# Cross-attention on one core: normalization in two halves, an earlier transposition of the probabilities, and two buffers for x

## The chip, the core and the metric

The kernel runs on one core of a Trainium2 chip. A core has five engines with a queue of instructions each: TensorE (PE, matrix products; its weight loads are listed as PEld), VectorE (DVE), ScalarE (ACT), GpSimd (POOL) and SyncE (SP), which here only issues DMAs. Each queue runs in order; engines wait for one another through semaphores. Sixteen DMA engines move data between the chip's memory (DRAM) and the on-chip memory; matrix products land in PSUM, eight banks of 2 KB per partition. The metric is the device time of one execution in microseconds (us). The time before is 1811.44 us, the median of three runs (1804.13 to 1816.82).

## The reference

A cross-attention block: 32 batches of 512 queries with 640 channels, 20 heads of 32 channels, and 77 context rows of 1024 channels for each batch. The reference also has weights for three further groups of context rows (object, others, ip), but the context has only the 77 text rows, so those groups are empty and add nothing.

```python
q = _heads(x @ to_q_w)                                # 32 x 512 x 640
k, v = _heads(ctx @ to_k_w), _heads(ctx @ to_v_w)     # 32 x 77 x 1024 -> 640
s = jnp.einsum('bhqd,bhkd->bhqk', q, k) / sqrt(32)
p = jax.nn.softmax(s, axis=-1)
h = _merge(jnp.einsum('bhqk,bhkd->bhqd', p, v))
out = h @ to_out_w + to_out_b + x
```

All data is 32-bit. The products with weights are made more exact by splitting both operands into a high and a low part and adding three products (high x high, high x low, low x high).

## The kernel before

**First stage (to about 250 us).** Twelve matmuls on zeros (line 253) start PE. Keys and values of all batches are computed in groups of 512 context rows (lines 177 to 220) and put into DRAM (`k_dram`, `v_dram`). The split weights of the output projection go to DRAM as well and come back later (`wos`, line 592). The values of the last group are computed inside the first two slots (`beside`).

**Slots.** The main part is a list of 160 slots, `slot(n)` for n = 0 to 159. Slot n handles batch b = n // 5 and the chunk j = n % 5 of 128 channels, which is four heads. The order of instructions is written out by hand: the program text of `slot` is the order on each engine. In a slot, in program order:

- `scores(n)` (line 410): 32 small matmuls into four PSUM tiles `sc`, one for each head, 512 queries as four blocks t of 128 partitions.
- `values(n - 3)` (line 478): probabilities (`raw`, keys in partitions) times values, for a chunk three slots back (`LAG`), into the one PSUM tile `pa`.
- `maxima(n)` (line 422): DVE takes the row maxima of the four heads.
- DMA issues on SP: `load_p(n - 2)` (line 470) reloads the probabilities of chunk n - 2 from DRAM; then keys, values of the batch, x, the residual (`xr`, line 504), as the slot has them.
- `add_bias` (line 508) on POOL, on a residual loaded a slot or more before.
- `piece` (line 515): the first half of the slot's share of the output projection of an earlier batch.
- `exps` (line 432) on ACT: for heads 0 and 1, 8 instructions with the row sums as a second result; they write `pn`, a tile of 128 x 16 x 80 with rows t * 4 + head, one of two by the parity of n.
- `transpose_p(n - 1)` (lines 454 and 461): DVE transposes the previous chunk's normalized probabilities in 32 x 32 blocks into the single tile `z`; then SP issues four DMAs that write it to a DRAM tile `pd` with keys as rows.
- `finish` (lines 544 to 550): DVE adds PSUM and residual for each block of the output that a piece has closed; SP stores complete rows. A block is 128 queries by 320 channels; the tables `STEPS` and `CUTS` say which piece closes which. In slots with j = 0, 1 and 3 the second piece closes one block, with j = 2 and 4 none; an output row is complete behind the second piece where j is 0 or 1.
- `transpose_x` (line 235) on DVE for j = 0 and 1: x of the next batch, in place in its buffer `xs`.
- `queries(n + 1)` (line 393): 15 matmuls for the next chunk's queries; `copy_q` (line 402) takes them to `qt`, on ACT, or on DVE in the first seven slots (`filling`: batches whose output projection has not begun).
- `exps` for heads 2 and 3, then `sums` (line 442, DVE reciprocal of all 16 row sums) and `normalize` (line 447, POOL multiplies all of `pn`, 1232 elements in each partition).
- `high_a`, `low_a` (lines 492 and 497): ACT and DVE split the values product.
- the second piece, `split_x` for j = 2 and 3 (lines 242 and 243, ACT high part, POOL low part, five chunks c of the next batch's x into `xt`), the remaining `transpose_x`, and `finish`.

`xs` has one buffer and `xt` seven tiles of one chunk each. All four quarters of the x of batch b + 2 are loaded in slot j = 4 of batch b. After the last slot, `end` transposes and reloads what is left and finishes the last projection.

The lines that set the order around the change are in `slot`, lines 585 to 640; in it `turns` holds what `transpose_x` is called for and `taken` is n - 3.

Of the kernel before, what the change touches and what calls it, by code (L numbers as in the profile page):

```python
# [8 lines left out]
F32 = mybir.dt.float32  # L9
# [28 lines left out]
def kernel(  # L38
# [185 lines left out]
    def load_x(b, quarters=range(4)):  # L224

        if b not in xss:
            xss[b] = xpool[0].tile([P, S // Q, C // 4], F32, tag="xs", name="xs")
        xs = xss[b]
        src = x[b].rearrange("(a j) (q u) -> q j a u", j=Q, q=4)
        for q in quarters:  # L230
            nc.sync.dma_start(xs[q * Q : (q + 1) * Q, :, :], src[q])  # L231

    def transpose_x(b, i):
        part = xss[b][:, 4 * i : 4 * i + 4, :].rearrange("p a u -> p (a u)")
        nc.vector.transpose(part, part)  # L235

    def split_x(b, c, high=nc.scalar.copy, low=nc.gpsimd):

        xt = xpool[0].tile([P, 2, S], FPR, tag="xt", name="xt", bufs=7)
        src = xss[b].rearrange("p (a t) u -> p t a u", t=NQ)[:, :, :, c * Q : (c + 1) * Q]  # L240
        parts = [xt[:, i, :].rearrange("p (t a j) -> p t a j", t=NQ, j=Q) for i in range(2)]
        high(parts[0], src)  # L242
        low.tensor_tensor(parts[1], src, parts[0].bitcast(F32), ALU.subtract)  # L243
        xts[b, c] = xt
# [4 lines left out]
    zero = kvt.tile([P, G], FPR, name="zero")  # L249
    nc.vector.memset(zero.bitcast(F32), 0.0)  # L250
    warm = psk.tile([P, G], F32, tag="ps", name="warm")
    for _ in range(12):
        nc.tensor.matmul(warm, zero[:, :P], zero, start=True, stop=True)

    def first(*ks):
# [106 lines left out]


    main = ctx.enter_context(tc.tile_pool(name="main", bufs=1, reuse_waits="tile"))
    ps = ctx.enter_context(tc.tile_pool(name="ps", bufs=1, space=PSUM, reuse_waits="tile"))
    psv = tc.alloc_tile_pool(name="psv", bufs=3, space=PSUM, side="right", reuse_waits="tile")
    late = []
# [10 lines left out]
        nc.gpsimd.memset(pn, 0.0)  # L378
        pnb.append(pn)
    qts = [main.tile([P, S], F32, name=f"qt{n}") for n in range(2)]  # L380
    z = main.tile([P, NBLK, NQ, Q], F32, name="z")
    def load_keys(b):
        nc.sync.dma_start(kbs[b % 2], k_dram[:, :, b * NKEY : (b + 1) * NKEY])

# [34 lines left out]
    def maxima(n):  # L419
        nms[n] = main.tile([P, HPC, NQ], F32, tag="nm", name="nm", bufs=2)  # L420
        for i, sc in enumerate(scs[n]):
            nc.vector.tensor_reduce(  # L422
                nms[n][:, i], sc[:, :, :NKEY], AX.X, ALU.max, negate=True
            )
# [12 lines left out]
                accum_out=sms[n][:, at : at + 1],  # L437
            )

    def sums(n):  # L440
        rss[n] = main.tile([P, NQ * HPC], F32, tag="rs", name="rs", bufs=2)
        nc.vector.reciprocal(rss[n], sms.pop(n))  # L442

    def normalize(n):
        rs = rss.pop(n)
        pf = pnb[n % 2][:, :, :NKEY]
        nc.gpsimd.tensor_tensor(  # L447
            pf, pf, rs.unsqueeze(2).to_broadcast([P, NQ * HPC, NKEY]), ALU.mult
        )

    def transpose_p(n):

        pn = pnb[n % 2]
        nc.vector.transpose(  # L454
            z.rearrange("p b t j -> p t b j"),
            pn.rearrange("p (t h) k -> p t (h k)", t=NQ).rearrange("p t (b i) -> p t b i", i=Q),
        )
        pd = dram.tile([NBLK * Q, S], F32, tag="pd", name="pd", bufs=6)
        rows = pd.rearrange("(b i) q -> i b q", i=Q)
        for a in range(4):  # L460
            nc.sync.dma_start(  # L461
                rows[:, :, a * P : (a + 1) * P],
                z[a * Q : (a + 1) * Q].rearrange("p b t j -> p b (t j)"),
            )
        pds[n] = pd

    def load_p(n):
        pd = pds.pop(n)
        raw = late[0].tile([KPAD, HPC, S], F32, tag="raw", name="raw", bufs=2)
        nc.sync.dma_start(raw, pd.rearrange("(h k) q -> k h q", h=HPC))  # L470
        raws[n] = raw
# [87 lines left out]
    PIECES = {2: (1, 0), 3: (1, 2), 4: (1, 4), 0: (2, 6), 1: (2, 8)}  # L559
    RESIDUAL = {1: (1, 0), 2: (1, 1), 3: (1, 2), 4: (1, 3)}  # L560
    BIAS = {2: (1, 0), 3: (1, 1), 4: (1, 2), 0: (2, 3)}
    TRANSPOSE_X = {0: ((0,), (1,)), 1: ((2,), (3,))}
    SPLIT_X = {2: (0, 1), 3: (2, 3, 4)}

    WO = {1: (0, 1, 2), 2: (3,), 3: (4,)}
# [2 lines left out]
    def take(m):  # L568
        values(m)
        high_a(m)  # L570
        low_a(m)

    def slot(n, beside=()):
        b, j = divmod(n, NC_)
        ahead, more = n + 1 < N, b + 1 < B
        back, first = PIECES[j]
        bo_, has_out = b - back, b >= back
        xsplits = SPLIT_X.get(j, ()) if more and n > LATE else ()
        turns = TRANSPOSE_X.get(j, ((), ())) if more and b else ((), ())
        if b == 1 and j < 2:  # L580
            turns = (((), ()), ((0, 1), (2, 3)))[j]
        taken = takes.get(n)
        filling = not has_out

        scores(n)
        if taken is not None:
            values(taken)
        maxima(n)
        if n - LAG + 1 in pds and n > LATE:
            load_p(n - LAG + 1)  # L590
        for k in WO.get(n, ()):
            nc.sync.dma_start(wos[0][:, k].bitcast(F32), wo_dram[:, k].bitcast(F32))
        if j == 0 and more:
            load_keys(b + 1)
        if j == 1:
            load_values(b)
        if n == NC_:
            load_x(b + 1, (2, 3))
        if j == 4 and b and b + 2 < B:
            load_x(b + 2, (0, 1))  # L600
        if j in RESIDUAL and b >= RESIDUAL[j][0]:
            load_residual(b - RESIDUAL[j][0], RESIDUAL[j][1])
        if j in BIAS and b >= BIAS[j][0]:
            add_bias(b - BIAS[j][0], BIAS[j][1])
        if has_out:
            piece(bo_, first)
        for i in range(2):
            exps(n, i)
        if n:
            transpose_p(n - 1)  # L610
        finish()
        if j == 4 and b + 2 < B:
            load_x(b + 2, (0, 1) if not b else (2, 3))
        for i in turns[0]:
            transpose_x(b + 1, i)
        if len(beside) > 1:
            context_values(LAST, beside[1], psv)
        if ahead:
            queries(n + 1)
        if len(beside) > 0:  # L620
            context_values(LAST, beside[0], psv)
        if filling and ahead:
            copy_q(n + 1, nc.vector.tensor_copy)
        for i in range(2, HPC):
            exps(n, i)
        sums(n)
        normalize(n)
        if taken is not None:
            high_a(taken)
        if has_out and ahead:  # L630
            copy_q(n + 1)
        if has_out:
            piece(bo_, first + 1)
        if taken is not None:
            low_a(taken)
        for c in xsplits:
            split_x(b + 1, c)
        for i in turns[1]:
            transpose_x(b + 1, i)
        finish()  # L640

    def end():


        last = B - 1
        load_p(N - 2)
        add_bias(last - 1, 3)
        piece(last - 1, 6)
        finish()
        transpose_p(N - 1)  # L650
        load_p(N - 1)
        load_residual(last, 0)
        load_residual(last, 1)
        piece(last - 1, 7)
        finish()
        take(N - 3)
        piece(last - 1, 8)
        piece(last - 1, 9)
        finish()
        load_residual(last, 2)  # L660

        def begin(i, j0, j1):
            t, h = divmod(i, 2)
            if j0 == 0:
                if i < 4:
                    pos[last, t, h] = ps.tile([P, S], F32, tag="sc", name="po", bufs=4)
                elif i == 4:
                    pos[last, t, h] = ps.tile([P, S], F32, tag="pq", name="po", bufs=1)
                elif i < 7:
                    output_bank(last, t, h)  # L670
                else:
                    pos[last, t, h] = late[1].tile([P, S], F32, tag="pa", name="po", bufs=1)
            for j in range(j0, j1):
                project(last, t, h, j)

        for i in range(2):
            begin(i, 0, 2)
        take(N - 2)
        for t in (0, 1, 2):
            add_bias(last, t)  # L680
# [88 lines left out]
```

## Time and profile before

| | us |
|---|---|
| median of three runs | 1811.44 |
| lowest and highest | 1804.13, 1816.82 |
| the profiled execution | 1809.79 |
| its span (first to last instruction) | 1808.0 |
| mean granted clock of PE in it | 0.987 |
| ACT, exponentials waiting for maxima (line 432) | 379.6 |
| POOL, normalization waiting for the reciprocal (line 447) | 659.9 |
| POOL, bias waiting for the residual (line 508) | 85.9 |
| DVE, transposition of x waiting for its load (line 235) | 74.2 |
| SP, x load waiting for the split of x (line 231) | 67.8 |

The lower rows are idle time of an engine just before the named work, summed, with what ended it. Idle time of an engine that is not the bottleneck costs nothing by itself. In rows of the profile, `L447 POOL` is the instruction of line 447 on GpSimd, `pn<-pn,rs` its output and inputs, and `x160` its count; in a timeline the first two numbers are start and duration in us, and the bracket holds the engine's idle time before it and what ended that. `SPq` is the queue of SyncE that issues DMAs. The granted clock is 1 at full speed.

### The profile page before, as it was taken

To read this page: it belongs to the slowest core of one execution; us is meant where nothing else is said; L and a number is where in the kernel's file an instruction comes from. 1 tells how busy PE (TensorE), PEld (TensorE's weight loads), DVE (VectorE), ACT (ScalarE), POOL (GpSimd) and SP (SyncE) were. 2 spreads that over 40 slices of the span, in tenths; PEclk is the share of its full clock that TensorE was granted. 3 is DMA by queue.
4 is the path that set the end of the run, shared out by engine and by line. 5 is a ranking of instruction groups with operands and counts; after the bars stand their busy time and mean duration, and the time that the engine had idled before them with its cause. 6 is when DMAs were issued, how large, how long until landed. Compare 5 with 4: busy or idle time off the path is not lost.

```text
span 1808.0 us, 39341 instructions
## 1 busy us (share of the span) xinstructions
PE 1763.3 (98%) x13852; PEld 1440.0 (80%) x13852; DVE 933.3 (52%) x1651; ACT 1108.9 (61%) x5698; POOL 789.7 (44%) x502
## 2 busy tenths in 40 slices
PE   8999998899999999999999999999999999999999
PEld 7888896678878888877788777888788888877787
DVE  5233134555555555555555555555555555545553
ACT  3132035666767777767677776677676777666662
POOL 0000034444445555545555545545555555535453
PEclk9999999999999999999999999999999999999999
DMA  9746465899999999998999999998899999898987
GB/s 186 149 94 174 105 168 138 211 231 235 232 232 239 232 243 235 240 235 219 237 232 237 228 230 237 230 233 230 229 234 230 229 240 237 229 224 219 236 207 202
DMA packets 465173, 389.12 MB, mean 215 GB/s; under 512 B 91280, under 2 KB 372368, under 8 KB 464976
## 3 DMA queue, kind: packets, MB, share of 16 engines
q1 hardware_dynamic: 462384, 379.49, 84.5%
q0 software_dynamic: 2496, 6.97, 1.3%
q8 instruction: 109, 1.79, 0.4%
q14 instruction: 88, 0.72, 0.1%
q10 hardware_dynamic: 96, 0.16, 0.0%
HBM read 223.82 MB, written 162.70 MB: 214 GB/s over the span
## 4 chain that ended last, share of the span: by engine, by line
PE 63%; DMA 17%; ACT 6%; POOL 6%; SPq 4%; DVE 2%; issue 2%; POOLq 0%; DVEq 0%; ACTq 0%
PE po L515 20%; PE pq L393 17%; PE pk L177 7%; PE pv L177 7%; DMA raw<-pd 6%; DMA pd<-z 6%; ACT pn L432 6%; PE sc L410 5%; PE pa L478 5%; POOL xt L243 4%; DMA xs<-in_x_dram 4%; SPq L461 2%; POOL pn L447 1%; SPq L231 1%; DVE xs L235 1%
## 5 line engine op out<-in xcount | busy, mean ns | idle before, releaser
L432 ACT ACTIVATE pn<-sc,nm 128x77 f32<-128x77 f32 x2560 | 787.4, 361 | 400.2 <-DVE nm L422 379.6
L515 PEld LDWEIGHTS po<-wo_s,at 128*128 128x128 f32 x3840 | 582.7, 190 | 143.8 <-issue 132.1
L447 POOL TENSOR_TENSOR pn<-pn,rs 128x1232 f32<-128x1232 f32 x160 | 364.0, 2275 | 665.1 <-DVE rs L442 659.9
L515 PE MATMUL po<-wo_s,at 128*128 128x320 f32 x3840 | 636.8, 316 | 0.0
L432 ACT ACTIVATION_READ_ACCUMULATOR pn<-sc,nm 128x1 f32 x2560 | 618.7, 242 | 0.0
L393 PE MATMUL pq<-xt,wq_s 128*128 128x512 f32 x2400 | 582.8, 395 | 0.0
L393 PEld LDWEIGHTS pq<-xt,wq_s 128*128 128x128 f32 x2400 | 450.1, 190 | 92.8 <-issue 4.9
L422 DVE TENSOR_REDUCE nm<-sc 128x4 f32<-128x308 f32 x640 | 261.0, 469 | 202.2 <-PE sc L410 202.1
L454 DVE STREAM_TRANSPOSE z<-pn 128x1280 f32<-128x1280 f32 x160 | 241.1, 1507 | 97.8 <-DMA pd<-z 92.3
L508 POOL TENSOR_TENSOR xr<-xr,bias 128x640 f32<-128x640 f32 x128 | 200.8, 1569 | 94.2 <-DMA xr<-in_x_dram 85.9
L243 POOL TENSOR_TENSOR xt<-xs,xt 128x512 fp32r<-128x512 f32 x160 | 200.0, 1274 | 35.6 <-ACT xt L242 35.6
L478 PE MATMUL pa<-raw,vb 80*32 80x512 f32 x1280 | 173.4, 613 | 27.6 <-DMA raw<-pd 19.6
L410 PEld LDWEIGHTS sc<-kb,qt 32*128 32x128 f32 x5120 | 157.5, 186 | 41.0 <-issue 35.1
L410 PE MATMUL sc<-kb,qt 32*128 32x77 f32 x5120 | 181.0, 277 | 8.7 <-DVE rs L442 5.8
L544 DVE TENSOR_TENSOR xr<-po,xr 128x320 f32<-128x320 f32 x256 | 117.5, 469 | 79.4 <-PE po L515 75.7
L235 DVE STREAM_TRANSPOSE xs<-xs 128x640 f32<-128x640 f32 x128 | 105.8, 832 | 74.2 <-DMA xs<-in_x_dram 74.2
L442 DVE RECIPROCAL rs<-sm 128x16 f32<-128x16 f32 x160 | 38.8, 243 | 196.3 <-ACT pn L432 196.3
L177 PE MATMUL pk<-ct,wk_s 128*128 128x512 f32 (+1 forms) x600 | 136.0, 387 | 3.1 <-ACT wk_s L89 3.1
L402 ACT COPY qt<-pq 128x512 f32<-128x512 f32 x153 | 93.3, 610 | 72.5 <-PE pq L393 72.1
L177 PE MATMUL pv<-ct,wv_s 128*128 128x512 f32 (+1 forms) x600 | 133.9, 381 | 0.0
L177 PEld LDWEIGHTS pk<-ct,wk_s 128*128 128x128 f32 x600 | 114.2, 191 | 23.2 <-ACT wk_s L89 3.6
L497 DVE TENSOR_TENSOR at<-pa,at 128x512 fp32r<-128x512 f32 x160 | 108.6, 679 | 37.2 <-ACT at L492 37.1
(31 smaller groups left out, 536.7 us busy)
## 6 DMA issues: line engine op xcount, KB each, us to landing
pd<-z SPq DMA_DIRECT2D x640, 160.0 KB, 5.4
raw<-pd SPq DMA_DIRECT2D x160, 640.0 KB, 5.5
xs<-in_x_dram SPq DMA_DIRECT2D x128, 320.0 KB, 6.0
xr<-in_x_dram SPq DMA_DIRECT2D x128, 320.0 KB, 5.7
out_dram<-xr SPq DMA_DIRECT2D x127, 320.0 KB, 3.9
vb<-v_dram SPq DMA_DIRECT2D x32, 200.0 KB, 6.0
kb<-k_dram SPq DMA_DIRECT2D x32, 192.5 KB, 7.3
cs<-in_ctx_dram SPq DMA_DIRECT2D x12, 512.0 KB, 9.4
```

Of the source, the lines that this page charges most:

```text
L177: nc.tensor.matmul(held[j][:, :gn], w[:, k, a, :], cts[g, k][:, c, :gn], start=(k == 0 and n == 0), stop=(k == NK - 1 and n == 2),)
L235: nc.vector.transpose(part, part)
L243: low.tensor_tensor(parts[1], src, parts[0].bitcast(F32), ALU.subtract)
L393: nc.tensor.matmul(pqs[n], wq_s[:, k, a, j * P : (j + 1) * P], xts[b, k][:, c, :], start=(k == 0 and m == 0), stop=(k == NC_ - 1 and m == 2),)
L410: nc.tensor.matmul(sc[:, t, :NKEY], qts[n % 2][r, t * P : (t + 1) * P], kbs[b % 2][r, j, :], start=True, stop=True, tile_position=(i * HD, 0),
L422: nc.vector.tensor_reduce(nms[n][:, i], sc[:, :, :NKEY], AX.X, ALU.max, negate=True)
L432: nc.scalar.activation(pnb[n % 2][:, at, :NKEY], sc[:, t, :NKEY], AF.Exp, bias=nms[n][:, i, t : t + 1], accum_out=sms[n][:, at : at + 1],)
L447: nc.gpsimd.tensor_tensor(pf, pf, rs.unsqueeze(2).to_broadcast([P, NQ * HPC, NKEY]), ALU.mult)
L454: nc.vector.transpose(z.rearrange("p b t j -> p t b j"), pn.rearrange("p (t h) k -> p t (h k)", t=NQ).rearrange("p t (b i) -> p t b i", i=Q),)
L478: nc.tensor.matmul(pas[n][i * HD : (i + 1) * HD, :], vb[:, i, :], raw[:, i, :], start=True, stop=True, tile_position=(0, i * HD),)
L508: nc.gpsimd.tensor_tensor(xrs[b, t], xrs[b, t], bias, ALU.add)
L515: nc.tensor.matmul(pos[b, t, h][:, :HALF], ats[b * NC_ + j][:, a, t * P : (t + 1) * P], wos[0][:, j, c, h * HALF : (h + 1) * HALF], start= ...
```

## The change

Eight edits in one version:

- `normalize(n, half)` takes the place of `sums` and `normalize`. Each half is a reciprocal of eight row sums and a POOL multiplication of two heads (616 elements in each partition). The first half stands behind the exponentials of heads 0 and 1, the second behind those of heads 2 and 3.
- `z` becomes two tiles. Where the projection runs (`has_out`, from slot 7), `transpose_p(n)` stands at the end of slot n, ahead of the last `finish`. In the slots before, `transpose_p(n - 1)` stands behind `maxima(n)`, and its DMAs ahead of the slot's other loads except the reload.
- `load_p` is issued ahead of the maxima; the order on SP is not changed by that.
- `xs` has two buffers. x of batch b + 2 is loaded a quarter at a time, in slots j = 1 to 4 of batch b (for batch 2: half in slot 4, half in slot 5).
- chunks 2 to 4 of odd batches go into three tiles of a new tag `xu`.
- chunks 2, 3 and 4 of batch 1 are split in slots 0, 1 and 2 instead of all in slot 3. All of `transpose_x` stands behind the first `finish`.
- in the slots before the projection runs, `values` stands behind `queries`.
- 22 matmuls on zeros instead of 12.

```diff
-            xss[b] = xpool[0].tile([P, S // Q, C // 4], F32, tag="xs", name="xs")
+            xss[b] = xpool[0].tile([P, S // Q, C // 4], F32, tag="xs", name="xs", bufs=2)
...
-        xt = xpool[0].tile([P, 2, S], FPR, tag="xt", name="xt", bufs=7)
+        if b % 2 and c > 1:
+            xt = xpool[1].tile([P, 2, S], FPR, tag="xu", name="xu", bufs=3)
+        else:
+            xt = xpool[0].tile([P, 2, S], FPR, tag="xt", name="xt", bufs=7)
...
-    for _ in range(12):
+    for _ in range(22):
         nc.tensor.matmul(warm, zero[:, :P], zero, start=True, stop=True)
...
-    z = main.tile([P, NBLK, NQ, Q], F32, name="z")
+    zs = [main.tile([P, NBLK, NQ, Q], F32, name=f"z{n}") for n in range(2)]
...
-    def sums(n):
-        rss[n] = main.tile([P, NQ * HPC], F32, tag="rs", name="rs", bufs=2)
-        nc.vector.reciprocal(rss[n], sms.pop(n))
-
-    def normalize(n):
-        rs = rss.pop(n)
-        pf = pnb[n % 2][:, :, :NKEY]
+    def normalize(n, half):
+        if half == 0:
+            rss[n] = main.tile([P, NQ, HPC], F32, tag="rs", name="rs", bufs=2)
+        heads = slice(2 * half, 2 * half + 2)
+        rs = rss[n][:, :, heads]
+        nc.vector.reciprocal(rs, sms[n].rearrange("p (t h) -> p t h", h=HPC)[:, :, heads])
+        pf = pnb[n % 2].rearrange("p (t h) k -> p t h k", h=HPC)[:, :, heads, :NKEY]
         nc.gpsimd.tensor_tensor(
-            pf, pf, rs.unsqueeze(2).to_broadcast([P, NQ * HPC, NKEY]), ALU.mult
+            pf, pf, rs.unsqueeze(3).to_broadcast([P, NQ, 2, NKEY]), ALU.mult
         )
...
-        pn = pnb[n % 2]
+        pn, z = pnb[n % 2], zs[n % 2]
...
-        xsplits = SPLIT_X.get(j, ()) if more and n > LATE else ()
+        xsplits = (SPLIT_X if b else {0: (2,), 1: (3,), 2: (4,)}).get(j, ()) if more else ()
...
         scores(n)
-        if taken is not None:
+        if taken is not None and has_out:
             values(taken)
-        maxima(n)
         if n - LAG + 1 in pds and n > LATE:
             load_p(n - LAG + 1)
+        maxima(n)
+        if n and n - 1 not in pds:
+            transpose_p(n - 1)
...
-        if n == NC_:
-            load_x(b + 1, (2, 3))
-        if j == 4 and b and b + 2 < B:
-            load_x(b + 2, (0, 1))
+        if b + 2 < B:
+            quarters = {4: (0, 1), 5: (2, 3)}.get(n, ()) if n <= NC_ else (j - 1,) if j else ()
+            if quarters:
+                load_x(2 if n <= NC_ else b + 2, quarters)
...
         for i in range(2):
             exps(n, i)
-        if n:
-            transpose_p(n - 1)
+        normalize(n, 0)
         finish()
-        if j == 4 and b + 2 < B:
-            load_x(b + 2, (0, 1) if not b else (2, 3))
-        for i in turns[0]:
+        for i in turns:
             transpose_x(b + 1, i)
...
             queries(n + 1)
+        if taken is not None and not has_out:
+            values(taken)
...
         for i in range(2, HPC):
             exps(n, i)
-        sums(n)
-        normalize(n)
+        normalize(n, 1)
...
         for c in xsplits:
             split_x(b + 1, c)
-        for i in turns[1]:
-            transpose_x(b + 1, i)
+        if has_out:
+            transpose_p(n)
         finish()
```

In `end`, the transposition of the last chunk is gone (it stands at the end of its slot), and the reload of that chunk stands behind two loads of residuals and a piece.

More of the change, by code (lines that the diff above doesn't have):

```diff
@@ L364 @@
     main = ctx.enter_context(tc.tile_pool(name="main", bufs=1, reuse_waits="tile"))
+    xpool.append(main)
     ps = ctx.enter_context(tc.tile_pool(name="ps", bufs=1, space=PSUM, reuse_waits="tile"))
@@ L561 @@
     BIAS = {2: (1, 0), 3: (1, 1), 4: (1, 2), 0: (2, 3)}
-    TRANSPOSE_X = {0: ((0,), (1,)), 1: ((2,), (3,))}
+    TRANSPOSE_X = {0: (0, 1), 1: (2, 3)}
     SPLIT_X = {2: (0, 1), 3: (2, 3, 4)}
@@ L577, in slot @@
         bo_, has_out = b - back, b >= back
-        xsplits = SPLIT_X.get(j, ()) if more and n > LATE else ()
-        turns = TRANSPOSE_X.get(j, ((), ())) if more and b else ((), ())
+        xsplits = (SPLIT_X if b else {0: (2,), 1: (3,), 2: (4,)}).get(j, ()) if more else ()
+        turns = TRANSPOSE_X.get(j, ()) if more and b else ()
         if b == 1 and j < 2:
-            turns = (((), ()), ((0, 1), (2, 3)))[j]
+            turns = ((), range(NQ))[j]
         taken = takes.get(n)
-        filling = not has_out
         scores(n)
-        if taken is not None:
+        if taken is not None and has_out:
             values(taken)
-        maxima(n)
         if n - LAG + 1 in pds and n > LATE:
             load_p(n - LAG + 1)
+        maxima(n)
+        if n and n - 1 not in pds:
+            transpose_p(n - 1)
         for k in WO.get(n, ()):
@@ L619, in slot @@
             queries(n + 1)
+        if taken is not None and not has_out:
+            values(taken)
         if len(beside) > 0:
             context_values(LAST, beside[0], psv)
-        if filling and ahead:
+        if ahead and not has_out:
             copy_q(n + 1, nc.vector.tensor_copy)
@@ L649, in end @@
         finish()
-        transpose_p(N - 1)
-        load_p(N - 1)
         load_residual(last, 0)
@@ L655, in end @@
         finish()
+        load_p(N - 1)
         take(N - 3)
```

## The prediction

> **What bounds the kernel now.** I read the page first, then busy time by stage, the timeline of two undisturbed slots, the chain of waits and the waits of TensorE (PE) and of the DMA issuer (SPq). The page and the stages (PE, its weight loads, DVE, ACT, POOL, granted clock, DMA share, GB/s):
>
> ```profile
> PE 1763.3 (98%) x13852; PEld 1440.0 (80%) x13852; DVE 933.3 (52%) x1651; ACT 1108.9 (61%) x5698; POOL 789.7 (44%) x502
> ...
> 0.00:25.00 25.00, 20.42 (x70) 16.05 (x71) 12.40 (x21) 9.35 (x17) 4.33 (x12) 0.86 1.03 186
> 264.62:345.17 80.55, 66.63 (x514) 51.48 (x513) 37.48 (x67) 45.94 (x268) 36.14 (x31) 0.92 0.69 160
> 345.17:1770.00 1424.83, 1402.43 (x11931) 1139.29 (x11930) 791.30 (x1416) 991.19 (x5282) 715.34 (x422) 0.99 0.91 232
> ```
>
> PE has work almost throughout, so only its gaps and its slow clock can be won. The third stage runs from the scores of slot 8 to those of slot 159: 151 slots in 1424.83 us, 9.44 each. An undisturbed slot, scores to scores:
>
> ```profile
> 1049.54 1.13 PE L410 MATMUL sc<-kb,qt 32*128 32x77 f32 x32
> 1050.69 1.64 DVE L422 TENSOR_REDUCE nm<-sc 128x4 f32<-128x308 f32 x4 [2.41 <-PE sc L410]
> 1051.26 0.33 ACT L432 ACTIVATE pn<-sc,nm 128x77 f32<-128x77 f32 x1 [1.69 <-DVE nm L422]
> 1055.98 0.29 ACT L432 ACTIVATION_READ_ACCUMULATOR pn<-sc,nm 128x1 f32 x1
> 1056.31 0.25 DVE L442 RECIPROCAL rs<-sm 128x16 f32<-128x16 f32 x1 [1.51 <-ACT pn L432]
> 1056.70 2.28 POOL L447 TENSOR_TENSOR pn<-pn,rs 128x1232 f32<-128x1232 f32 x1 [2.92 <-DVE rs L442]
> 1058.73 1.13 PE L410 MATMUL sc<-kb,qt 32*128 32x77 f32 x32
> ```
>
> 1058.73 - 1049.54 = 9.19 us. So 1424.83 - 151 x 9.19 = 37 us are excess: 22.4 is PE idle (1424.83 - 1402.43), the other 14.7 mostly slower clock after it (0.99 of 1425 us). The reason stands in the chain, here between two slots, and in the waits from 450 to 1800 us and of the issuer:
>
> ```profile
> 1012.10 3.77 POOL xt L243 x3
> ...
> 1019.01 6.65 DMA pd<-z
> ...
> 1025.74 6.33 DMA raw<-pd
> ...
> 1032.21 1.07 PE pa L478 x8
> ```
>
> ```profile
> PE pa L478 <- DMA raw<-pd: 15.6, 14, 3.1
> SPq L470 <- DMA pd<-z: 385.3, 304, 4.7
> ```
>
> Every fifth slot the x load waits for the last split of x on GpSimd (one x buffer). On the same in-order queue the write of the probabilities stands behind it, then their reload, and PE's values product waits for that. The reload also waits 385 us in all for the write to land.
>
> **Part by part: the steady loop.** First, x. Two buffers take the x load off the split: the buffer written in batch b was last read in batch b-1. The loads are spread, one quarter in each of slots 1 to 4 instead of four in slot 4. The extra tiles (tag xu) make each batch's splits independent of the previous batch's queries; ACT reaches these splits only behind a copy of the queries anyway, so I count nothing for them. Instructions and bytes stay the same.
>
> Second, the transposition. It moves from behind slot n+1's first exponentials to the end of slot n. What is queued behind it on DVE is the second finish and the four maxima of slot n+1, on which ACT waits. This closes a loop DVE, ACT, DVE, POOL, DVE whose length I need:
>
> ```profile
> 292.53 2.29 POOL L447 TENSOR_TENSOR pn<-pn,rs 128x1232 f32<-128x1232 f32 x1
> 294.85 1.51 DVE L454 STREAM_TRANSPOSE z<-pn 128x1280 f32<-128x1280 f32 x1 [1.70 <-POOL pn L447]
> L508 POOL TENSOR_TENSOR xr<-xr,bias 128x640 f32<-128x640 f32 x128 | 200.8, 1569 | 94.2 <-DMA xr<-in_x_dram 85.9
> L243 POOL TENSOR_TENSOR xt<-xs,xt 128x512 fp32r<-128x512 f32 x160 | 200.0, 1274 | 35.6 <-ACT xt L242 35.6
> L544 DVE TENSOR_TENSOR xr<-po,xr 128x320 f32<-128x320 f32 x256 | 117.5, 469 | 79.4 <-PE po L515 75.7
> ```
>
> No trace shows a half normalization (616 elements a partition). The two whole-operand rows give 2.305 ns per element and 0.09 us fixed ((1569-1274)/128 elements). The same fixed part on the broadcast row gives (2.28-0.09)/2 + 0.09 = 1.18. The ends are 1.14 (half of 2.28) and 1.51 (616 x 2.305 + 0.09); I take 1.18, the row of the same operation. The reciprocal doubles (0.25 more on DVE), its first half lying under ACT's second half of exponentials.
>
> From the maxima's start: reciprocal at +5.62 (1056.31), POOL at +6.01 (1056.70), done +7.19, transposition from +7.22 (0.03 behind POOL in the rows) to +8.73, with one finish (0.47) +9.20. Slots 0, 1 and 3 of a batch have one closing block in their second piece, slots 2 and 4 none: 3 x 9.20 + 2 x 8.73 = 45.1 us a batch against PE's 5 x 9.19 = 45.95. The loop fits, by 0.9 us a batch; it becomes the bound if a half costs over 1.36. At 1.51 it is 46.7: 0.75 x 30 batches = 23 us. GpSimd's other work keeps out of the way: in slots 2 and 3 the splits stand behind the second half, and slot 4's bias (1.57) behind three splits (3.8) ends 5.4 us after 7.19, at 12.6, where that slot's first half is ready at 9.2 + 3.5 (0.57 to the first exponential, half of 5.0, reciprocal 0.25, 0.14) = 12.7. That cover has no spare, but the second half starts 2.5 later and the first needs 1.2 of it. Were a bias late by more than 1.3, the loop would wear the rest.
>
> Third, two z buffers remove DVE's wait for the write (92.3 us), counted for the fill alone:
>
> ```profile
> L454 DVE STREAM_TRANSPOSE z<-pn 128x1280 f32<-128x1280 f32 x160 | 241.1, 1507 | 97.8 <-DMA pd<-z 92.3
> ...
> L235 DVE STREAM_TRANSPOSE xs<-xs 128x640 f32<-128x640 f32 x128 | 105.8, 832 | 74.2 <-DMA xs<-in_x_dram 74.2
> ```
>
> The second row is the transposition of x, which in slots 0 and 1 now stands twice before the second reciprocal: maxima, reciprocal half, one finish and two of 0.83 end at 3.5 + 0.5 + 1.7 = 5.7 after the maxima's start, where 5.6 is wanted. Its wait for x (74.2 us) should go, since each quarter is now issued a slot or more ahead.
>
> Fourth, the queue. Per slot:
>
> ```profile
> pd<-z SPq DMA_DIRECT2D x640, 160.0 KB, 5.4
> raw<-pd SPq DMA_DIRECT2D x160, 640.0 KB, 5.5
> xs<-in_x_dram SPq DMA_DIRECT2D x128, 320.0 KB, 6.0
> xr<-in_x_dram SPq DMA_DIRECT2D x128, 320.0 KB, 5.7
> out_dram<-xr SPq DMA_DIRECT2D x127, 320.0 KB, 3.9
> DMA to landing us min/median/max: 4.7/5.5/8.1
> 1054.05 2.42 SPq L461 DMA_DIRECT2D pd<-z  x4
> ```
>
> The landing row is that of raw. Counted from slot n's scores, z is ready at 1.15 + 8.73 = 9.9, that is 0.7 into slot n+1. Four writes issue in 2.4 (0.6 each); after slots 0 and 1 an output store follows; so a reload is issued 3.1 to 3.7 into the slot. It no longer waits for its own write, issued a whole slot earlier. PE wants it after the next scores, at 9.19 + 1.13 = 10.3. At the median it lands at 8.6 to 9.2, at the maximum at 11.2 to 11.8. Bytes: 1.31 MB a slot for pd and raw, and 12 transfers of 0.33 and 0.4 of keys and values a batch, 10.9 MB; in 45.95 us this is 237 GB/s, where the stage row's 232 at share 0.91 means about 255 at full share. Slot 1 carries 2.5 MB (an output, x, residual and values beside pd and raw), 9.8 us at 255, so slot 2's reload starts behind 0.6 us of backlog. I let it and jitter keep 0.4 us a batch, 12 of the 37: the steady loop gives 25 (ends 37 and, with the half at 1.51 too, about 0).
>
> The Trainium skill's page "DMA: Bandwidth & Descriptors", section "Queues, rings and completion order", says that on each DMA engine descriptors are consumed in ring order. This speaks against the change: the reload, now issued right behind the four writes, would start behind their bytes, and by this rule its landing lies towards the row's maximum, which is the first rival; the spread from 4.7 to 8.1 agrees that what stands ahead matters, without showing how much.
>
> **Start and fill.**
>
> ```profile
> 1.46 4.58 PE L253 MATMUL warm<-zero 128*128 128x512 f32 x12 [1.46 <-DVE zero L250]
> 9.16 6.43 PE L177 MATMUL pk<-ct,wk_s 128*128 128x512 f32 x15 [3.12 <-ACT wk_s L89]
> 17.49 3.56 PE L177 MATMUL pk<-ct,wk_s 128*128 128x512 f32 x15
> 297.64 1.13 PE L410 MATMUL sc<-kb,qt 32*128 32x77 f32 x32 [0.87 <-DVE qt L402]
> 304.86 1.13 PE L410 MATMUL sc<-kb,qt 32*128 32x77 f32 x32 [1.47 <-DVE rs L442]
> 308.38 1.77 PE L478 MATMUL pa<-raw,vb 80*32 80x512 f32 x8 [2.39 <-DMA raw<-pd]
> 315.52 1.13 PE L410 MATMUL sc<-kb,qt 32*128 32x77 f32 x32 [0.83 <-issue]
> 331.10 1.51 DVE L454 STREAM_TRANSPOSE z<-pn 128x1280 f32<-128x1280 f32 x1 [5.54 <-DMA pd<-z]
> ```
>
> After 12 warm-up matmuls PE idles 3.12 us and its first 15 real ones take 6.43 instead of 3.56 (clock 0.86 over this stage). Ten more at 3.56/15 = 0.24 end at 8.4, leaving 0.8 idle: gain 2.9. At 4.58/12 = 0.38 they end at 9.9 and cost 0.7; the later ones run warm, so I take 2.9.
>
> In the fill, slot 3 takes 7.22 and slot 4 10.66, as the late reload holds the queries. Values behind queries frees these: 3.4. In slot 6 DVE's transposition waits 5.54 for z, with the query copy behind it; the second z removes that wait, but four x transpositions instead of two now stand there: 5.5 - 2 x 0.83 = 3.9, of which I count the two thirds that I count of the 37, 2.6. Sum 6, of 13.9 idle and 6.4 slow clock in that stage (ends 0 and 20). The end's transposition moves up too; PE is busy there: nothing.
>
> Sum: 25 + 2.9 + 6 = 34 off 1809.8 (span 1808.0 and 1.8 around it): 1776. The profiled run is 1.6 below the median, 1811.4, which changes nothing.
>
> **Rivals.** *The reload becomes the wait in every slot (slower).* If T is the slot, z at 9.9, then 2.4 + 0.6 of issue and a landing L must be over by 2T + 1.13: T = (11.8 + L)/2. At the median T is below 9.19 and PE decides; it passes today's 9.44 at L = 7.1. At 7.6, T is 9.7: 151 x 0.26 = 40 us more, 1850, the time of this rival; at 8.1, 1885. For: the order of issue. Against: the median, and that x no longer comes in a burst of 1.3 MB. Chance 0.12.
>
> *The halves do not run apart (slower).* ACT must write heads 2 and 3 while POOL scales 0 and 1 in interleaved rows of one tile. If the program makes ACT wait for that, its second half starts after 2.5 + 0.25 + 0.14 + 1.18 instead of 2.5: 1.6 more in a loop of 9.0 on average, 10.6, so 151 x 1.16 over today: 1985. No pair in this trace has such a pattern. Chance 0.07.
>
> *The gain is hidden anyway.* At 93% of the rate seen, the DMA engines keep today's waits in another place and only start and fill gain: 1809.8 - 9 = 1801, or up to 1812 where those gain nothing either. For: share 0.91 already. Chance 0.16.
>
> **Numbers.** Forecast 0.65, 1776, with its own range 1762 (all 37 and 8 of the fill) to 1795 (6 of the 37). A measurement here tells about 1%, 18 us. Faster 0.65, same 0.16, slower 0.19. The range takes in the hidden case, 1762 to 1812, leaving the slower ones out.
>
> **What would show it.** Right: PE's wait for raw below 5 us, transposition starting under 0.1 after POOL's second half, the first 15 real matmuls near 3.6, slots at 9.2. Wrong: a POOL half over 1.36; maxima starting over 1.2 after the scores in most slots; reloads landing over 7 us after issue; ACT idle between heads 1 and 2.

## The result, and the profile after

The changed kernel takes 1890.74 us (median of 4 runs, 1889.28 to 1904.76) against 1808.7 (4 runs, 1804.13 to 1816.82): a ratio of 1.0466, 95% interval 1.0402 to 1.053. It is slower, where 1776 was forecast. The profiled run took 1891.13, 81.3 more than the profiled run before.

The page of the changed kernel: busy time, the main DMA queue, the chain by engine, the groups of the normalization, the transposition, the bias and the values product, and the landing times.

```profile
span 1889.4 us, 40159 instructions
...
PE 1793.9 (95%) x13862; PEld 1458.9 (77%) x13862; DVE 960.5 (51%) x1811; ACT 1110.4 (59%) x5698; POOL 820.2 (43%) x662
...
q1 hardware_dynamic: 462384, 379.49, 90.2%
...
PE 73%; DMA 16%; ACT 4%; SPq 3%; DVE 2%; issue 1%; POOL 1%; ACTq 0%; DVEq 0%; POOLq 0%
...
L451 POOL TENSOR_TENSOR pn<-pn,rs 128x616 f32<-128x616 f32 x320 | 392.6, 1231 | 390.5 <-DVE rs L449 386.5
...
L512 POOL TENSOR_TENSOR xr<-xr,bias 128x640 f32<-128x640 f32 x128 | 201.7, 1576 | 352.8 <-DMA xr<-in_x_dram 335.2
...
L458 DVE STREAM_TRANSPOSE z<-pn 128x1280 f32<-128x1280 f32 x160 | 241.8, 1511 | 116.3 <-POOL pn L451 114.6
...
L482 PE MATMUL pa<-raw,vb 80*32 80x512 f32 x1280 | 178.6, 630 | 73.1 <-DMA raw<-pd 57.4
...
raw<-pd SPq DMA_DIRECT2D x160, 640.0 KB, 7.3
```

The queue's bytes are those of before (379.49 MB), but the chain that ended last now holds 16% of DMA, and the reload (raw) takes 7.3 us from issue to landing where it took 5.5. DVE's wait for the landed write is gone (the transposition now waits for POOL), so that step did what it says.

Busy time by stage, the same three stages as in the prediction (PE, PEld, DVE, ACT, POOL, granted clock, DMA share, GB/s):

```profile
0.00:25.00 25.00, 23.42 (x89) 18.56 (x90) 12.30 (x21) 9.36 (x17) 4.33 (x12) 1.00 1.05 188
262.43:343.28 80.85, 65.21 (x513) 51.39 (x512) 40.30 (x76) 45.87 (x268) 37.96 (x39) 0.92 0.82 199
343.28:1847.76 1504.48, 1433.47 (x11930) 1157.49 (x11930) 817.05 (x1567) 992.65 (x5282) 743.99 (x573) 0.97 0.97 218
```

The first scores come at 262.43 instead of 264.62 (-2.2), the fill takes 80.85 instead of 80.55 (+0.3), the steady loop 1504.48 instead of 1424.83 (+79.6), and what follows slot 159's scores 41.6 instead of 38.0 (+3.6): together the 81.3 by which the spans differ. The steady loop is the matter. Its excess over 151 x 9.19 rose from 37 to 117 us: 71 us of PE idle (1504.48 - 1433.47) and 46 of slower clock.

The slots say where. From scores to scores, means over slots 8 to 158 by the slot's place in its batch (j), worked out from the trace:

| place | 0 | 1 | 2 | 3 | 4 |
|---|---|---|---|---|---|
| before | 9.19 | 10.42 | 9.19 | 9.19 | 9.19 |
| after | 9.31 | 9.28 | 12.05 | 9.94 | 9.24 |

The loss of slot 1 (1.2 us a batch) is gone, as forecast; slot 2 lost 2.9 and slot 3 0.75. One batch's slots 0, 1 and 2 (slots 80 to 82 of the kernel) by busy time, then the chain there.

```profile
1064.29:1073.48 9.19, 9.19 (x80) 7.47 (x79) 6.05 (x12) 6.08 (x34) 4.04 (x3) 1.00 1.01 245
1073.48:1082.68 9.20, 9.20 (x80) 7.47 (x79) 6.47 (x13) 6.08 (x34) 2.46 (x2) 1.00 0.80 177
1082.68:1097.23 14.55, 12.12 (x80) 9.41 (x79) 5.33 (x10) 7.07 (x36) 4.34 (x4) 0.77 1.11 218
```

```profile
1075.61 1.72 PE po L519 x11
1077.34 8.77 DMA raw<-pd
1086.11 0.14 issue
1086.24 1.93 PE pa L482 x8
```

The reload issued at 1077.34 lands 8.8 us later; PE, ready for it 1.13 after the scores of 1082.68, starts its values product at 1086.24. That slot lasts 14.55 us, with 2.43 of it idle and the rest of the excess in a clock of 0.77. The issuer's timeline (start, duration, operation) in the slot before, slot 81, which issued that reload:

```profile
1074.23 2.19 SPq L465 DMA_DIRECT2D pd<-z  x4
1076.52 0.71 SPq L554 DMA_DIRECT2D out_dram<-xr  x1
1077.34 0.80 SPq L474 DMA_DIRECT2D raw<-pd  x1
1078.18 0.59 SPq L390 DMA_DIRECT2D vb<-v_dram  x1
1078.88 0.44 SPq L231 DMA_DIRECT2D xs<-in_x_dram  x1
1079.37 0.55 SPq L508 DMA_DIRECT2D xr<-in_x_dram  x1
1083.42 2.47 SPq L465 DMA_DIRECT2D pd<-z  x4
```

From 1079.9 to 1083.4 SP issues nothing. Its waits over the whole run:

```profile
SPq L465 <- DVE z L458: 657.7, 154, 6.3
```

That is what the end-of-slot transposition does to the queue: SP waits 657.7 us for the new z, with every transfer of the slot either out already or queued behind the four writes. Before, SP waited for the write to land instead (385.3). These are a write and a store of slot 83 (place 3) in the kernel before, and that chunk's reload in slot 84:

```profile
1054.05 2.42 SPq L461 DMA_DIRECT2D pd<-z  x4
1056.57 0.66 SPq L550 DMA_DIRECT2D out_dram<-xr  x1
1060.98 0.30 SPq L470 DMA_DIRECT2D raw<-pd  x1
1062.72 0.85 SPq L231 DMA_DIRECT2D xs<-in_x_dram  x2
```

There the reload was issued only when its own write had landed (at 1060.90), with nothing but the store still in flight. In the changed kernel it stands directly behind four writes and a store. For the reload of slot 1 the traces give both parts (medians over the loop, each by itself). Before, 320 KB were in flight when it was issued; they had landed after 0.67 us, and the reload 4.83 us later. In the changed kernel it was 800 KB, landed after 3.49 us, and the reload 5.03 us later. So nearly all of the longer landing is time in which what stood ahead had not landed. What was issued within 3 us behind the reload did not grow: 1000 KB before, 840 KB after.

### The profile page after: what moved, and what is told of

It is laid out like the page before. It is cut to its first block, busy times and chain, and to the rows that moved or that the text cites. A ratio compares the mean times of both kernels' runs of the same rounds, so it can differ in the third digit from the quotient of the medians.

```text
span 1889.4 us, 40159 instructions
## 1 busy us (share of the span) xinstructions
PE 1793.9 (95%) x13862; PEld 1458.9 (77%) x13862; DVE 960.5 (51%) x1811; ACT 1110.4 (59%) x5698; POOL 820.2 (43%) x662
## 3 DMA queue, kind: packets, MB, share of 16 engines
q1 hardware_dynamic: 462384, 379.49, 90.2%
q0 software_dynamic: 2496, 6.97, 1.2%
## 4 chain that ended last, share of the span: by engine, by line
PE 73%; DMA 16%; ACT 4%; SPq 3%; DVE 2%; issue 1%; POOL 1%; ACTq 0%; DVEq 0%; POOLq 0%
PE po L519 25%; PE pq L397 21%; DMA raw<-pd 13%; PE pa L482 7%; PE pv L177 7%; PE pk L177 7%; PE sc L414 6%; ACT pn L436 4%; DMA vb<-v_dram 2%; SPq L465 2%; DVE z L458 1%; POOL pn L451 1%; DVE nm L426 1%; SPq L554 0%; DMA xr<-in_x_dram 0%
## 5 line engine op out<-in xcount | busy, mean ns | idle before, releaser
L519 PEld LDWEIGHTS po<-wo_s,at 128*128 128x128 f32 x3840 | 597.4, 194 | 153.7 <-issue 138.7
L519 PE MATMUL po<-wo_s,at 128*128 128x320 f32 x3840 | 652.8, 321 | 1.9 <-DVE xr L548 1.9
L451 POOL TENSOR_TENSOR pn<-pn,rs 128x616 f32<-128x616 f32 x320 | 392.6, 1231 | 390.5 <-DVE rs L449 386.5
L397 PE MATMUL pq<-xt,wq_s 128*128 128x512 f32 x1680 | 419.7, 397 | 0.0
L397 PEld LDWEIGHTS pq<-xt,wq_s 128*128 128x128 f32 x1680 | 316.0, 192 | 59.4
L449 DVE RECIPROCAL rs<-sm 128x8 f32<-128x8 f32 x320 | 64.9, 203 | 442.9 <-ACT pn L436 442.4
L482 PE MATMUL pa<-raw,vb 80*32 80x512 f32 x1280 | 178.6, 630 | 73.1 <-DMA raw<-pd 57.4
L246 POOL TENSOR_TENSOR xt<-xs,xt 128x512 fp32r<-128x512 f32 x112 | 140.1, 1276 | 96.9 <-ACT xt L245 96.9
L397 PE MATMUL pq<-xu,wq_s 128*128 128x512 f32 x720 | 180.8, 394 | 0.0
L397 PEld LDWEIGHTS pq<-xu,wq_s 128*128 128x128 f32 x720 | 134.9, 187 | 32.6
```

The source lines that it names most:

```text
L397: nc.tensor.matmul(pqs[n], wq_s[:, k, a, j * P : (j + 1) * P], xts[b, k][:, c, :], start=(k == 0 and m == 0), stop=(k == NC_ - 1 and m == 2),)
L451: nc.gpsimd.tensor_tensor(pf, pf, rs.unsqueeze(3).to_broadcast([P, NQ, 2, NKEY]), ALU.mult)
L482: nc.tensor.matmul(pas[n][i * HD : (i + 1) * HD, :], vb[:, i, :], raw[:, i, :], start=True, stop=True, tile_position=(0, i * HD),)
L519: nc.tensor.matmul(pos[b, t, h][:, :HALF], ats[b * NC_ + j][:, a, t * P : (t + 1) * P], wos[0][:, j, c, h * HALF : (h + 1) * HALF], start= ...
```

## The experiments

Two theories at first. **Order:** the reload is late because it is issued behind the wait for z, the writes and the store; moving it alone cures the loss. **Bytes or engines:** x's new place, the late bias or the longer DVE-POOL loop does it. The first four expectations call their theories Q (slot 1's transfers crowd the queue, so its reload lands late) and P (with the transposition at the slot's end the DMA engines run empty while SP waits, and the lost rate is the bound). In each diff "-" is the changed kernel unless said otherwise.

**Slot 1's quarter of x moved to slot 0** (`x_off_slot1`).

```diff
-            quarters = {4: (0, 1), 5: (2, 3)}.get(n, ()) if n <= NC_ else (j - 1,) if j else ()
+            quarters = {4: (0, 1), 5: (2, 3)}.get(n, ()) if n <= NC_ else (j - 1,) if b == 1 else {0: (0,), 2: (1,), 3: (2,), 4: (3,)}.get(j, ())
```

> The changed kernel with one edit: the quarter of x that was loaded in slot 1 of a batch is loaded in slot 0. Theory Q (queue of slot 1): slot 1 issues an output, the reload, the values, a quarter of x and a residual close together, the reload and the residual land late (8.8 and 10.6 us), so the scores of slot 2 to those of slot 3 take 12.1 us instead of 9.2. Without x there slot 2 falls to 10.5 or less and the time to 1805 to 1845. Theory P (position): with the transposition at the slot's end the DMA queue runs empty while SP waits for z, the lost rate is the bound, and a batch keeps at least 49 us wherever x is loaded: 1870 to 1895.

1876.38 us, ratio 1.0399 (1.0315 to 1.0483): 0.6% less than the changed kernel, inside the intervals. Slot 2 still took 11.2, slot 3 10.1. The time is in the range of P; x's quarter in slot 1 is a small part at most.

**The transposition back behind the next slot's first exponentials** (`transposition_back`), all else as changed.

```diff
+        if has_out:
+            transpose_p(n - 1)
...
-        if has_out:
-            transpose_p(n)
```

> The changed kernel with the transposition of the probabilities back where it was (in the next slot, behind its first exponentials); halves, two z, two x, spread loads and the fill stay. P: the DMA queue is filled ahead again, the waits for the reload nearly vanish, 1765 to 1800. Q: slot 1 still carries the same bytes, so slot 2 stays 1 us or more over 9.2: 1800 to 1850.

1829.55, ratio 1.0139 (1.0096 to 1.0183). The long slot 2, which Q expected to stay, is gone. PE's wait for the reload, which P expected nearly to vanish, is 28 us (57 in the changed kernel). It is 1.4% slower than the kernel before, with slots of 9.24 to 9.97. Its SP waits:

```profile
SPq L474 <- DMA pd<-z: 584.6, 320, 6.8
```

The reload waits for the landing of its write as before, and longer (584.6 against 385.3). Which edit does that, `x_only` tells below.

**The bias behind the second half of the normalization** (`bias_later`).

```diff
-        if j in BIAS and b >= BIAS[j][0]:
-            add_bias(b - BIAS[j][0], BIAS[j][1])
...
         normalize(n, 1)
+        if j in BIAS and b >= BIAS[j][0]:
+            add_bias(b - BIAS[j][0], BIAS[j][1])
```

> The changed kernel with the bias behind the second half of the normalization instead of ahead of the first on GpSimd. Q with a second step (the late residual holds the bias, the bias the normalization, this the transposition and the next write): slot 3 falls from 9.96 to 9.3, slot 2 keeps 2 us or more: 1855 to 1875. P, or the second step being covered: within 8 us of 1891.

1896.45, ratio 1.051 (1.0393 to 1.0627), slot 2 at 11.95: no effect. In the changed kernel POOL idles 335 us for the residual ahead of the bias; here 11.8, and the time stays. That idle time costs nothing measurable here.

**The reload alone ahead of the wait for z** (`reload_early`): slot n, behind its loads, reloads the chunk n-1, a slot sooner in the queue's order. `load_p(N - 2)` in the end, then without work, goes.

```diff
+        if n > NC_ + 2 and n - 1 in pds:
+            load_p(n - 1)
         if has_out:
             piece(bo_, first)
...
-        load_p(N - 2)
```

> The changed kernel with the reload one slot earlier: in slot n, behind the other loads and ahead of the wait for z, SP reloads chunk n - 1, whose write was issued at the slot's start. Same DMAs, same bytes. Q: PE's wait for the reload falls from 57 us to under 10, what is left is the bias behind a late residual: 1780 to 1830. P: the rate is the bound, the wait turns up elsewhere: 1860 or more.

1778.97, ratio 0.9859 (0.9811 to 0.9907) to the kernel before: the loss is gone and 1.4% gained. Its page:

```profile
PE 1757.4 (99%) x13862; PEld 1432.2 (80%) x13862; DVE 959.6 (54%) x1811; ACT 1109.3 (62%) x5698; POOL 821.5 (46%) x662
...
PE 96%; DMA 1%; ACT 1%; DVE 1%; SPq 0%; issue 0%; POOL 0%; DVEq 0%; ACTq 0%; POOLq 0%
...
raw<-pd SPq DMA_DIRECT2D x160, 640.0 KB, 5.9
```

Its steady loop:

```profile
342.52:1736.08 1393.56, 1393.56 (x11930) 1128.48 (x11930) 815.00 (x1566) 991.40 (x5282) 746.12 (x574) 1.00 0.95 236
```

PE is busy for all of the 1393.56 us, 9.23 a slot, at full clock, though the DMA engines move 236 GB/s and slot 1 carries the same bytes. The issuer in a slot 1 (scores at 1062.29):

```profile
1062.98 2.30 SPq L465 DMA_DIRECT2D pd<-z  x4
1065.39 0.58 SPq L554 DMA_DIRECT2D out_dram<-xr  x1
1066.30 0.54 SPq L390 DMA_DIRECT2D vb<-v_dram  x1
1066.95 0.51 SPq L231 DMA_DIRECT2D xs<-in_x_dram  x1
1067.52 0.67 SPq L508 DMA_DIRECT2D xr<-in_x_dram  x1
1068.87 0.32 SPq L474 DMA_DIRECT2D raw<-pd  x1
1072.24 2.38 SPq L465 DMA_DIRECT2D pd<-z  x4
```

The reload goes out in the time in which SP waits for z, and has over a slot in hand: a landing of 8 us, as in this place still, harms nobody. The reload waits for its own write again there (240 us of SP in all), but PE wants the chunk only in the next slot but one. The order theory stands, and P falls: the transposition is still at the slot's end.

**x alone, in the kernel before** (`x_only`; "-" is the kernel before): two x buffers and a quarter in each of slots 1 to 4, without the extra tiles `xu`. The old loads of x go.

```diff
-            xss[b] = xpool[0].tile([P, S // Q, C // 4], F32, tag="xs", name="xs")
+            xss[b] = xpool[0].tile([P, S // Q, C // 4], F32, tag="xs", name="xs", bufs=2)
...
+            quarters = {4: (0, 1), 5: (2, 3)}.get(n, ()) if n <= NC_ else (j - 1,) if j else ()
```

> The kernel before with x alone changed: two buffers, a quarter in each of slots 1 to 4. Theory S (the spread load helps by itself, as the prediction counted): slot 1 falls from 10.35 to 9.3, 1765 to 1785. Theory O (order on SP: x and the residual are issued ahead of the slot's writes, the writes land later, and the reload that waits for them too, as the 1829 us with the transposition back suggest): 1800 to 1840, with the waits spread over all slots.

1843.51, ratio 1.0257 (1.0212 to 1.0301): slower by itself. Its issuer:

```profile
1018.80 0.30 SPq L470 DMA_DIRECT2D raw<-pd  x1
1019.16 0.46 SPq L231 DMA_DIRECT2D xs<-in_x_dram  x1
1019.67 0.48 SPq L504 DMA_DIRECT2D xr<-in_x_dram  x1
1020.37 2.66 SPq L461 DMA_DIRECT2D pd<-z  x4
1029.33 0.30 SPq L470 DMA_DIRECT2D raw<-pd  x1
```

In slots 1 to 4 reload, x and residual now stand ahead of the writes, and the next reload waits until those have landed: their landing takes 6.4 at the median (5.4 before), SP waits 617 us for it in all (385 before), and here it is 10.5 us from one reload to the next where PE needs 9.19. The time is 3.5 us over theory O's range. The loss is not spread over all slots, as O had it: slot 3 takes 10.99, slots 0 and 1 9.35 and 9.45, the others 9.2.

**x in one burst, in the changed order** (`x_burst`): all four quarters in slot 4.

```diff
-            quarters = {4: (0, 1), 5: (2, 3)}.get(n, ()) if n <= NC_ else (j - 1,) if j else ()
+            quarters = {4: (0, 1), 5: (2, 3)}.get(n, ()) if n <= NC_ else (0, 1) if j == 4 else ()
...
+        if n > NC_ and j == 4 and b + 2 < B:
+            load_x(b + 2, (2, 3))
```

> The changed kernel with all four quarters of x loaded in slot 4 again, still two buffers. If slot 2 is long because slot 1's x shares the DMA engines with its reload, slot 2 falls to 10 or less and another slot pays: 1840 to 1890, since the reload still stands behind the writes. If the spread itself made the loss: 1780 to 1820.

1955.26, ratio 1.0878 (1.0813 to 1.0944), slot 1 at 13.8: above both ranges. Slot 2 fell to 9.6, and slot 1, behind the burst, lost more than slot 2 gained. So spreading x costs 2.6% in the old order (with the second buffer) and saves 3.8% in the new one (1.0466/1.0878).

**One whole normalization** (`whole_norm`; "-" is `reload_early`).

```diff
-        normalize(n, 0)
...
-        normalize(n, 1)
+        normalize(n)
```

> The kernel with the early reload, but with one whole normalization of 2.28 us behind all exponentials instead of two halves. The loop from maxima to maxima then has 2.28 instead of 1.23 in it: 10.0 to 10.3 us with one finish, 9.6 to 9.8 without, so 1860 to 1930. If the halves are not what lets the loop fit: within 10 us of 1779.

1895.9, ratio 1.0548 (1.0501 to 1.0595), slots of 9.8 to 10.1. The head of its chain by line:

```profile
ACT pn L436 40%; POOL pn L449 18%; PE pv L177 7%; PE pk L177 7%; DVE nm L426 3%; DVE xr L546 2%; DVE rs L446 2%; PE po L517 2%; PE pq L397 1%; DMA xs<-in_x_dram 1%; DVE z L456 1%; SPq L463 0%; PE pa L480 0%; PE sc L414 0%; DMA xr<-in_x_dram 0%
```

Exponentials and normalization carry it: with the transposition at the slot's end the loop through DVE, ACT and POOL is too long unless the normalization is halved. The halves are worth 6.5% there (0.9859/1.0548).

**Fill and second finish mended as well** (`reload_early_2`; "-" is `reload_early`): the second finish behind the next maxima, and batch 2's transpositions of x at the end of slot 6.

```diff
+        finish()
...
-        for i in turns:
+        for i in turns if b > 1 else ():
             transpose_x(b + 1, i)
...
+        for i in turns if b == 1 else ():
+            transpose_x(b + 1, i)
...
-        finish()
```

> The early reload and two more edits: the slot's second finish behind the next maxima (0.45 out of the loop, so 9.26 us slots become 9.19: 6 us), and the four transpositions of batch 2's x at the end of slot 6 instead of ahead of the query copy (slot 6 from 15.5 to under 9, 6 to 10 us with the slow clock behind it). Expected 1760 to 1770.

1777.84, ratio 0.9891 (0.9848 to 0.9934): the same as `reload_early`. Slot 6 fell from 15.55 to 6.97, but slot 7 rose from 12.43 to 17.27; the steady slots stayed at 9.23, so the second finish is not what lengthens them from 9.19; what does stays open. In slot 7 DVE waits only 2.37 us for x, but PE's values product waits 4.61 us for a reload issued at 321.73: another wait took the place of the one for x.

**What stands behind the reload taken to another queue** (`loads_act`): values, x and residual issued by ACT about 8 us into the slot; the reload stays behind writes and store. The three calls of the loads move, unaltered but for the queue, into a function `loads`.

```diff
-            load_residual(b - RESIDUAL[j][0], RESIDUAL[j][1])
+            load_residual(b - RESIDUAL[j][0], RESIDUAL[j][1], queue=queue)
...
             copy_q(n + 1)
+        if n > 2 * NC_:
+            loads(n, nc.scalar)
```

> The changed kernel, but from slot 11 on the loads of values, x and residual are issued on ScalarE's queue behind the query copy (about 8 us into the slot; values one slot sooner, the bias behind the second half of the normalization as in the run bias_later, which alone changed nothing). The reload stays where the change put it, behind the four writes and the output store. Theory B (what is issued right behind the reload takes its share of the DMA engines): with nothing behind it the reload lands 5.5 to 6.2 us after issue at the median, slots 2 and 3 of a batch go from 12.06 and 9.96 to under 9.4, time 1775 to 1800. Theory A (what stands ahead of it counts: the writes, the output and the late issue): slot 1's reload still lands 8 us or more after issue, slot 2 stays above 11, time 1860 to 1895. In between, 1800 to 1860: both count.

1868.44, ratio 1.0327 (1.0292 to 1.0362). Slot 2 fell only to 11.23, and slot 1's reload still took 7.74 (8.17 in the changed kernel), with nothing issued within 3 us behind it. So for this reload what stands ahead decides. The loads issued behind it matter for the next one, slot 2's reload: that lands in 6.78 instead of 8.71, with 1280 KB in flight at its issue instead of 1600.

One rule orders these four kernels. PE wants a chunk 10.3 us after the scores of the slot that reloads it (9.19 + 1.13), or 1.13 after the next scores where the slot is longer. The table has the mean time of the reload's issue after its slot's scores plus its median landing, by the slot's place, from the traces (slots 8 to 158), and behind the arrow the mean length of the following slot:

| | 0 | 1 | 2 | 3 | 4 |
|---|---|---|---|---|---|
| before | 3.73 + 7.11 → 10.42 | 4.16 + 5.50 → 9.19 | 2.94 + 5.38 → 9.19 | 1.96 + 5.32 → 9.19 | 1.26 + 5.34 → 9.19 |
| after | 3.25 + 6.78 → 9.28 | 3.92 + 8.17 → 12.05 | 4.29 + 8.71 → 9.94 | 1.89 + 7.38 → 9.24 | 2.67 + 6.93 → 9.31 |
| transposition_back | 5.10 + 5.36 → 9.76 | 3.67 + 5.57 → 9.24 | 4.93 + 5.47 → 9.97 | 5.20 + 5.27 → 9.48 | 5.00 + 5.12 → 9.43 |
| loads_act | 3.49 + 6.60 → 9.39 | 3.95 + 7.74 → 11.23 | 4.01 + 6.78 → 9.61 | 1.30 + 6.62 → 9.24 | 2.93 + 6.58 → 9.31 |

Where the sum passes 10.3 (eight places), the next slot takes 9.48 to 12.05; where it does not, 9.19 to 9.43. Slot 1 before and after is the lesson: issued at nearly the same time (4.16 and 3.92), the reload took 2.7 us longer to land.

## Why the prediction was wrong

**The step that failed is "Fourth, the queue"**, in the sentence "At the median it lands at 8.6 to 9.2". The time of issue was about right: 3.1 to 3.7 into the slot was forecast, 1.9 to 4.3 measured, 3.9 in slot 1. The landing was not: I took the median of reloads (5.5) that had waited for their write to land, with little in flight ahead of most of them, and gave it to one that starts right behind four writes and a store. The removed wait turned into time in the queue: 7.3 at the median (its own sign of being wrong was "over 7 us"), 8.2 and 8.7 in slots 1 and 2. So slot 1's reload lands 12.1 us into the slot, where 9.2 was forecast and PE wants it at 10.3. The kernel before had the same thing in a row of its own: its reload of slot 0, behind the burst of x, took 7.11. The "0.6 us of backlog" ahead of slot 2's reload measured 4.5 us (1600 KB in flight), and the term "0.4 us a batch" measured 2.9 + 0.75 in slots 2 and 3.

The sentence on the Trainium skill's page "DMA: Bandwidth & Descriptors" (section "Queues, rings and completion order"), that descriptors are consumed in ring order, was the one to follow. These runs agree: slot 1's reload took 8.17 behind 800 KB and 5.50 behind 320 KB.

**The first rival named the mechanism** ("the reload becomes the wait in every slot", 0.12), with 1885 at a landing of 8.1. It was right in kind and not in place. At the measured median of 7.3 its formula gives T = 9.55, but the loss sits almost alone in slots 2 and 3, which follow slot 1's 2.5 MB, and two fifths of the loop's excess are slow clock (46 of 117), which the formula leaves out. That 1885 is near 1890.74 is a coincidence of the two.

**First, x.** The wait on the split went (no such row is left in SP's waits) and slot 1's loss with it. But the prediction let the spread itself cost nothing. That held in the new order alone; in the old one two buffers and the spread cost 2.6% (`x_only`).

**Second, the transposition.** Right: the half costs 1.231 where 1.18 was taken, and slots without a late reload last 9.19 to 9.26 against a loop of 9.20. The halves run apart: in slot 80 GpSimd scaled the first half from 1068.98 to 1070.21 while ScalarE went on with an exponential every 0.30 us. So the second rival (1985) fell; `whole_norm` shows that without them the loop decides. The bias comes late as feared, but POOL's spare time covers it (`bias_later`).

**Third, the two z buffers** removed DVE's wait, as forecast. What they are worth by themselves no run shows.

**Start, fill, end.** The warm-ups: -2.2 measured, -2.9 forecast. Two rows of the timeline show it, the first 15 real matmuls at 4.10 instead of 6.43 (3.6 was forecast), behind 22 warm-ups without a gap:

```profile
1.46 7.89 PE L256 MATMUL warm<-zero 128*128 128x512 f32 x22 [1.46 <-DVE zero L253]
9.32 4.10 PE L177 MATMUL pk<-ct,wk_s 128*128 128x512 f32 x15
```

The fill gave +0.3 where -6 was forecast. Slot 4 fell from 10.66 to 6.66 as expected, but slot 6 rose from 11.97 to 16.61 and slot 7 from 10.38 to 12.67. In slot 6:

```profile
326.86 3.02 DVE L235 STREAM_TRANSPOSE xs<-xs 128x640 f32<-128x640 f32 x4 [7.42 <-DMA xs<-in_x_dram]
...
329.81 0.65 DVE L406 COPY qt<-pq 128x512 f32<-128x512 f32 x1
...
330.61 2.00 PE L414 MATMUL sc<-kb,qt 32*128 32x77 f32 x32 [9.17 <-DVE rs L449]
```

The transpositions of x that I had counted by their duration (0.83 each) wait 7.42 us for x on DVE, with the query copy and so the next scores queued behind them (the profile names the reciprocal that follows the copy). I had written that this wait "should go" and had not followed the loads of batch 2's x through the fill, where the queue is behind: the last of the four was issued at 320.02 and landed at 326.77. The end, which I set at nothing, cost 3.6, and 5.4 in `reload_early`. Two gaps of PE that follow slot 159's scores in the changed kernel's timeline are 3.4 of it:

```profile
1858.10 1.15 PE L519 MATMUL po<-wo_s,at 128*128 128x320 f32 x6 [1.86 <-DVE xr L548]
...
1867.27 1.06 PE L482 MATMUL pa<-raw,vb 80*32 80x512 f32 x8 [1.55 <-DMA raw<-pd]
```

The kernel before shows no gap there. What makes the first stays open.

**The forecast of 1776 and the 1778.97 of `reload_early`** agree only in part for the reasons given: its steady loop gained 31.3 (25 forecast), its start 2.3, its fill 0.4 (6 forecast), and its end lost 5.4. That the sums lie so close is partly luck.

## What to carry to other kernels

A transfer's landing time belongs to what stands ahead of it when it is issued; if a change removes a wait that let the queue run empty, price the transfer by the bytes that now stand before it, not by the old median. On an in-order issuing queue, put a transfer whose data is ready ahead of an instruction that will wait: here that one move took the ratio from 1.0466 to 0.9859 with the same bytes. An edit's sign can hang on that order: the spread of x, with a second buffer, cost 2.6% in one order and saved 3.8% against a burst in the other.

## What the runs showed of the hardware

A short idle of PE can cost more than itself, but need not. In slot 82 of the changed kernel 2.43 us of waiting made a slot of 14.55 out of 9.20, as the granted clock fell to 0.77 over the slot (0.50 from 1087 to 1091). Slot 37 idled longer, 2.66 us, and its clock stayed at 1.00. Of the changed kernel's 45 slots with over 0.3 us of idle 19 had a clock under 0.95, in the kernel before 7 of 22, the shortest idle among these being 1.00 us; no slot with less idle had one. Over the steady loop 71 us of idle came with 46 of slow clock; with no idle (`reload_early`) the clock stayed at 1.00.

The issue of one reload took 0.30 us or more than twice that: 0.30 in the kernel before (at 1060.98, after a pause of SP), 0.80 in the changed one (at 1077.34, right behind the writes and the store). What is in flight does not explain it: at 1087.86, after a pause, it took 0.30 with four writes, a store and two loads not landed. What makes it stays open.

More engine share was not more work: the DMA share of the steady loop rose from 0.91 to 0.97 while the rate fell from 232 to 218 GB/s; in `reload_early` 0.95 came with 236.
